# A gated recurrence on one core: one of its six recurrent products of a step computed from three bf16 parts instead of in f32

## The chip, the core and the metric

The kernel runs on one core of a Trainium2 chip. The metric is the device time of one execution in microseconds; lower is better. A core has five engines with queues of their own: TensorE (PE in the profile; PEld is its weight loads), VectorE (DVE), ScalarE (ACT), GpSimd (POOL) and SyncE (SP, here for DMAs alone).

## The reference

For 8 sequences of 512 steps, with 512 inputs and 512 hidden units, all in f32:

```
r, z   = split(sigmoid([x_t, h] @ w_W + w_b))       # w_W: 1024 x 1024
hh     = h @ wh_W + wh_b                            # wh_W: 512 x 512
h_new  = z * h + (1 - z) * tanh(x_t @ wx_W + wx_b + r * hh)
out[:, t] = x_t + h_new
```

The products with x_t don't depend on h and can be made ahead. The three products with h (for r, z and hh) can't: each step needs the h of the step before.

## The kernel before

**Layout.** h lies with its units on partitions: four blocks k of 128 units, of which k = 0, 1 make half A and k = 2, 3 half B. In a product h is the stationary operand (the loaded weights: 128 partitions by 32 columns) and the weight matrix streams past it. 32 columns are a quarter of TensorE's width, so four such products, j = 0 to 3, go to four column groups and leave their results on PSUM partitions 32j to 32j + 31. Of the 32 columns only the 8 of the present step hold h (8 sequences); the others are zero, and a group of four steps (GS) fills one set of PSUM banks, on top of the x part that ScalarE has copied there (`spread`).

**Banks.** The outputs of a step are cut by half of the units and by gate. Bank A (192 columns per j) holds hh, z and r of half A. Bank B (128 columns) holds r and hh of half B. `cs` ("C", 64 columns) holds z of half B. For each bank there are 4 k times 4 j matmuls a step. `wa` and `wb` are the weights of h, read through `wh`.

**Order of a step.** A hand-written string sets TensorE's order:

```
ORDER = "A0 B0 A1 A2 A3 B1 B2 B3 C0 C1 C2 C3"
```

A letter is a bank and a digit a k, four matmuls each. Behind these comes `x_step`: a share of the x products of a later group, 384 columns in four steps of eight and 288 in the other four (`SHARE`), into the tiles `xp` and `eps`.

**The recurrence.** When a bank is done, VectorE turns it back to units on partitions by 32x32 transposes (`turn_r`, `turn_h`, `turn_z`), ScalarE applies the sigmoids, VectorE scans, ScalarE takes the tanh, VectorE scans again:

- `md0` and `md1` are the operands of the first scan (`memory`), interleaved in two slots: hh, then times r plus the x part. Its result is `m`, of 16 elements (8 sequences by 2 slots) for each k, and the tanh of it goes to slot 1 of the old h.
- `hd0` (0, -1, 1 - z) and the three slots of the old h make the second scan (`update`): its third slot is the new h. The tiles `hTA` and `hTB`, eight of each, hold the h of eight steps.

Half A goes ahead: its bank is done after A3, its new h is wanted at A0 and B0 of the next step, that of half B only at A2. POOL adds x to the new h for the output. The x sums that `x_step` needs are made beside (`odd`, `even`, `both`, `more`), three of them on VectorE in steps 2, 3 and 5 of each eight, behind the updates.

**What orders the engines.** The code records its operations in program order (class `Flow`); each engine runs its own in that order, and waits are put where a read, a write or a PSUM bank demands it. All instructions therefore carry one line in the profile (L227). `DVE_FILL` says how many of the first fills go to VectorE instead of POOL. `IDLE` makes two one-element memsets on VectorE at the end of each step (`idle`), and a third stands behind `turn_z(0)`.

Of the kernel before, what the change touches and what calls it, by code (L numbers as in the profile page):

```python
# [8 lines left out]
F32 = mybir.dt.float32  # L9
BF16 = mybir.dt.bfloat16  # L10
AF = mybir.ActivationFunctionType
ALU = mybir.AluOpType
# [10 lines left out]

DVE_FILL = 23
IDLE = 3
ORDER = "A0 B0 A1 A2 A3 B1 B2 B3 C0 C1 C2 C3"

FIRST = "A0 A1 A2 A3 x x x x B0 B1 B2 B3 C0 C1 C2 C3"

BANKS = {"A": 192, "B": 128, "C": 64}  # L30

# [17 lines left out]

XP = {"A": slice(0, 192), "X": slice(192, 320), "C": slice(320, 384), "B": slice(384, 512)}  # L50

# [35 lines left out]
class Flow:  # L87
# [44 lines left out]
    def plan(self):  # L132
# [9 lines left out]
        for i, item in enumerate(self.items):  # L142
# [71 lines left out]
            done.append(snap)  # L214

    def emit(self, tc):

# [21 lines left out]
def tile_cond_rnn_residual(  # L239
# [105 lines left out]
    def wh(bank, k, j):  # L345
        return wa[:, k, j] if bank == "A" else wb[:, k, j, {"C": slice(0, 64), "B": slice(64, 192)}[bank]]

# [7 lines left out]
    NH = 2 * GS  # L355
    hT = [[pair(n, f"hT{n}{i}", 32, 3) for i in range(NH)] for n in "AB"]

    md0 = [[pair(n, f"md0{n}{i}", 32, 2) for i in range(2)] for n in "AB"]
    md1 = [[pair(n, f"md1{n}{i}", 32, 2) for i in range(2)] for n in "AB"]
    hd0 = [[pair(n, f"hd0{n}{i}", B, 3) for i in range(2)] for n in "AB"]  # L360
# [10 lines left out]
    nc.scalar.activation(const.tile([P, 1], F32, name="table"), zeros[:, :1], AF.Sigmoid)  # L371
    for n, t_ in enumerate(hd0[0] + hd0[1] + md0[0] + md0[1] + hT[0] + hT[1]):
# [13 lines left out]
    def state(hf, i, slot=2):  # L386
# [8 lines left out]
         "B": wide[q]["B"][:, : BANKS["B"]],  # L395
         "C": cs[:, HU * q : HU * q + HU]}
# [11 lines left out]

    for t_ in [cs, banks[0]["A"], banks[0]["B"], banks[1]["A"]]:
        mm(t_, none, none[:, :1].broadcast_to([P, t_.shape[1]]), start=True)  # L410
# [42 lines left out]
    def turn_x(g, hf):  # L453

        c0 = XP["X"].start + HU * hf
        nc.vector.transpose(
            md1[hf][g % 2][:, :, :, 1].rearrange("p n c -> p c n"), source(g)[:, c0 : c0 + HU]
        )
# [97 lines left out]
    spread(0, "ABC")  # L556
    for hf in range(2):
# [7 lines left out]
    for i in range(T):  # L565
# [8 lines left out]
        for n in (ORDER if i else FIRST).split():  # L574
            if n == "x":
                take(first[3], 1)
                continue
            bank, k = n[0], int(n[1])
            hs = hT[k // 2][i % NH][:, :, k % 2, 2]
# [9 lines left out]
        def scan(c_, out_, d0, d1):  # L589
# [9 lines left out]
        raw = {  # L599
            "h": (pa[:, :HU], ps["B"][:, HU:]),  # L600
            "z": (pa[:, HU : 2 * HU], ps["C"]),
            "r": (pa[:, 2 * HU :], ps["B"][:, :HU]),
        }
# [9 lines left out]
        def turn_r(hf):  # L613
            tr, _ = turned("r", hf)
            r_done[hf] = act(md0[hf][g % 2][:, rows, :, 1].rearrange("p n c -> p c n"),
                tr,
                AF.Sigmoid,
            )

        def turn_h(hf):  # L620
            inst = nc.vector.transpose(
                md1[hf][g % 2][:, :, :, 0].rearrange("p n c -> p c n"), raw["h"][hf]
            ).ins
# [4 lines left out]
        def turn_z(hf):  # L628
# [10 lines left out]
        ms = [  # L639
            work.tile([P, 2, B, 2], F32, tag=f"m{hf}", name=f"m{hf}_{i}").rearrange("p c n s -> p n c s")  # L640
            for hf in range(2)
        ]

        def memory(hf, q):

            c_ = slice(q, q + 1)
            scan(c_, ms[hf], md0[hf][g % 2][:, rows], md1[hf][g % 2][:, rows])
            act(state(hf, i, 1)[:, :, c_], ms[hf][:, :, c_, 1], AF.Tanh)

# [28 lines left out]
        for hf in range(2):  # L678
            act(state(hf, i + 1, 0), state(hf, i + 1), AF.Copy)
        if i < 3:  # L680
            inst = load_x(i + 1)
# [8 lines left out]
        if o == LAST:  # L690
            if u == 2:
                spread(2 * o + 1, "AB")
                turn_x(2 * o + 1, 0)
                turn_x(2 * o + 1, 1)
            elif u == 3:
                spread(2 * o + 1, "C")
        elif u == 0:
# [8 lines left out]
        elif u == 1:  # L706
            if sums:
                nc.scalar.copy(more[HI], eps)
            spread(2 * o + 1, "BC" if o == 0 else "AC")
        elif u == 2:  # L710
# [25 lines left out]
        elif u == 7 and nxt:  # L736
            if o:
                nc.scalar.copy(odd[LO, XC], reg(GA))
            spread(2 * o + 2, "C")
            turn_x(2 * o + 2, 1)  # L740
# [109 lines left out]
```

## Time and profile before

| | |
|---|---|
| Time, median of 3 runs | 1655.47 us (1655.45 to 1658.25) |
| Profiled execution: time | 1657.46 us |
| Profiled execution: span, first to last instruction | 1655.7 us |
| Granted TensorE clock, mean | 0.999 |
| Busy: PE, PEld | 99%, 91% of the span |
| Busy: DVE, ACT, POOL | 70%, 72%, 18% of the span |
| DMA engines, mean over most of the span | under a tenth busy |

Busy time is the union of the modelled durations of instructions. In a group's row stand the line, engine, operation, output and inputs by the program's names, shapes as partitions by elements, the count, the busy microseconds, the mean nanoseconds of one, and the idle time of the engine just ahead of them with what ended it. In a row of the timeline stand the start and the length in microseconds, the instruction with the number that were merged into it, and in brackets the idle time before it. Each f32 matmul appears in the trace as two matmuls and two weight loads.

### The profile page before, as it was taken

Reading aid. Unit: us, or ns where it says so; the run is one execution under the profiler, and the core shown is the slowest. Engines: PE = TensorE matmul, PEld = TensorE weight load, DVE = VectorE, ACT = ScalarE, POOL = GpSimd, SP = SyncE. Lnnn points to the kernel's source line nnn. Section 1 sums busy time; section 2 is a strip of 40 time slices with the busy share of each in tenths; the row PEclk is TensorE's granted clock in tenths of the full one; section 3 lists DMA queues with packets and bytes.
Section 4 is the critical chain, followed back from the end, with each engine's and each line's share of the span. In section 5 each row is a group of like instructions: output and inputs, shape, how many; then the busy total and the mean of one; then the engine's idle time right before and its main releaser. Section 6 shows DMA issues by size and latency. Waiting matters only on the chain.

```text
span 1655.7 us, 125580 instructions
## 1 busy us (share of the span) xinstructions
PE 1645.6 (99%) x54298; PEld 1500.2 (91%) x54298; DVE 1153.9 (70%) x9194; ACT 1193.8 (72%) x5998; POOL 301.9 (18%) x1279
## 2 busy tenths in 40 slices
PE   9999999999999999999999999999999999999998
PEld 5999999999999999999999999999999999999987
DVE  6776676676766766767667767677676766766765
ACT  3777777777777777777777777777777777777775
POOL 1211111111111111111111111111111111111111
PEclk9999999999999999999999999999999999999999
DMA  4000000000000000000000000000000000000000
GB/s 182 11 18 14 15 15 16 16 14 15 16 15 15 14 16 16 14 14 15 16 15 14 14 17 14 15 14 17 14 14 15 17 14 14 15 17 10 10 10 10
DMA packets 37284, 31.14 MB, mean 19 GB/s; under 512 B 4084, under 2 KB 35060, under 8 KB 36600
## 3 DMA queue, kind: packets, MB, share of 16 engines
q1 hardware_dynamic: 36576, 22.89, 4.5%
q8 instruction: 424, 6.95, 1.7%
q14 instruction: 132, 1.08, 0.2%
q10 hardware_dynamic: 152, 0.22, 0.1%
HBM read 14.70 MB, written 8.39 MB: 14 GB/s over the span
## 4 chain that ended last, share of the span: by engine, by line
PE 99%; DVE 1%; issue 0%; ACT 0%; DVEq 0%; SPq 0%
PE A L227 40%; PE B L227 26%; PE xp L227 18%; PE cs L227 13%; PE eps L227 1%; DVE tr L227 0%; DVE m L227 0%; DVE tz L227 0%; DVE md1B L227 0%; DVE md1A L227 0%; DVE hTA L227 0%; DVE hTB L227 0%; ACT hTB L227 0%; DVE zeros L227 0%; DVE rows L227 0%
## 5 line engine op out<-in xcount | busy, mean ns | idle before, releaser
L227 PE MATMUL A<-wa,hTA 128*32 128x192 f32 x8192 | 559.5, 326 | 2.4 <-DVE hTA L227 2.2
L227 PE MATMUL B<-wb,hTA 128*32 128x128 f32 x8192 | 454.8, 273 | 0.0
L227 PE MATMUL A<-wa,hTB 128*32 128x192 f32 x8192 | 448.6, 326 | 0.0
L227 PEld LDWEIGHTS A<-wa,hTA 128*32 128x32 f32 x8192 | 292.5, 122 | 124.6 <-DVE hTA L227 101.7
L227 DVE STREAM_TRANSPOSE tr<-A 128x64 f32<-128x64 f32 x512 | 128.0, 250 | 367.6 <-PE A L227 367.6
L227 POOL TENSOR_TENSOR ot<-xin,hTB 128x16 f32<-128x16 f32 x495 | 123.8, 250 | 1290.4 <-DVE hTB L227 1290.4
L227 PEld LDWEIGHTS B<-wb,hTA 128*32 128x32 f32 x8192 | 352.6, 122 | 2.8 <-issue 0.3
L227 PE MATMUL B<-wb,hTB 128*32 128x128 f32 x8192 | 339.6, 273 | 0.0
L227 PEld LDWEIGHTS A<-wa,hTB 128*32 128x32 f32 x8192 | 330.4, 122 | 9.1 <-DVE hTB L227 0.2
L227 ACT ACTIVATE md0A<-tr 128x16 f32<-128x16 f32 x512 | 112.4, 219 | 238.5 <-DVE tr L227 238.4
L227 PE MATMUL xp<-tw,sx 128*32 128x384 f32 (+2 forms) x1464 | 269.7, 433 | 0.0
L227 PEld LDWEIGHTS B<-wb,hTB 128*32 128x32 f32 x8192 | 262.3, 122 | 0.2 <-issue 0.2
L227 PE MATMUL cs<-wb,hTB 128*32 128x64 f32 x8192 | 230.3, 219 | 0.4 <-issue 0.3
L227 PE MATMUL cs<-wb,hTA 128*32 128x64 f32 x8192 | 230.2, 219 | 0.0
L227 DVE TENSOR_TENSOR_SCAN hTB<-hd0B,hTB 128x24 f32<-128x24 f32 x1024 | 158.0, 196 | 99.8 <-ACT hTB L227 99.8
L227 PE MATMUL xp<-wx,xin 128*32 128x384 f32 (+4 forms) x1348 | 219.1, 413 | 0.0
L227 PEld LDWEIGHTS cs<-wb,hTA 128*32 128x32 f32 x8192 | 207.5, 122 | 0.0
L227 DVE TENSOR_TENSOR_SCAN hTA<-hd0A,hTA 128x24 f32<-128x24 f32 x1024 | 190.9, 186 | 0.0
L227 ACT ACTIVATE hd0B<-tz 128x16 f32<-128x16 f32 x512 | 115.6, 226 | 94.5 <-DVE tz L227 94.5
L227 PEld LDWEIGHTS cs<-wb,hTB 128*32 128x32 f32 x8192 | 180.2, 122 | 0.7 <-issue 0.7
L227 ACT ACTIVATE hTB<-hTB 128x16 f32<-128x16 f32 x512 | 120.3, 235 | 79.1 <-DVE hTB L227 72.8
L227 ACT ACTIVATE hTA<-m 128x8 f32<-128x8 f32 x1024 | 160.8, 206 | 0.6 <-DVE m L227 0.3
(101 smaller groups left out, 2680.6 us busy)
## 6 DMA issues: line engine op xcount, KB each, us to landing
out_dram<-ot SPq DMA_DIRECT2D x128, 64.0 KB, 1.6
xin<-in_x_dram SPq DMA_DIRECT2D x112, 64.0 KB, 2.4
wx<-in_wx_dram SPq DMA_DIRECT2D x4, 768.0 KB, 7.0
wa<-in_wa_dram SPq DMA_DIRECT2D x4, 384.0 KB, 9.8
wb<-in_wb_dram SPq DMA_DIRECT2D x1, 1152.0 KB, 13.7
xin<-in_x_dram SPq DMA_DIRECT2D x3, 256.0 KB, 3.7
wb<-in_wb_dram SPq DMA_DIRECT2D x1, 384.0 KB, 14.1
head<-in_xh_dram ACTq DMA_DIRECT2D x1, 208.0 KB, 4.7
```

The lines of the kernel that those rows point to most:

```text
L227: inst = getattr(self, item.op, getattr(engine, item.op, None))(*item.args, **item.kw)
```

## The change

Of half B, hh is now computed apart and in bf16; z and r of half B share bank B. In the string of the order "C" has become "H".

- **Products.** h is split into three bf16 parts (their sum is h), side by side as 24 stationary columns (3 parts by 8 sequences). The weights of hh are split as well: the upper half of each f32 word of `wb`, and the same of two remainders, `w2` and `w3`, which POOL makes in step 0. `parts` issues, for each k and j, one matmul with its weight load and two (`kept`) without a load of their own. The streamed operand is every second bf16 of f32 words. The first three steps (`PLAIN`) still use f32 for H.
- **Sums.** The three parts' results lie on 24 partitions of each 32 of `cs`, the bias on the other eight. The product starts afresh each step (`start=k == 0`), so ScalarE no longer fills that bank. The first scan of half B has five slots instead of two (`SL`), 40 elements for each k: three parts, the bias, then times r plus x.
- **Parts of h.** VectorE makes them by two subtractions behind the updates of half B, into `split` (two tiles). The halves of h are one tile of four k, `hT`.
- **Order.** Of half B, z is turned ahead of h's first update, and hh behind it. The two memsets at a step's end are gone (`IDLE = 1`), and `DVE_FILL` is 12.

```diff
-DVE_FILL = 23
-IDLE = 3
-ORDER = "A0 B0 A1 A2 A3 B1 B2 B3 C0 C1 C2 C3"
+DVE_FILL = 12
+IDLE = 1
+ORDER = "A0 B0 A1 A2 A3 B1 B2 B3 H0 H1 H2 H3"
...
-BANKS = {"A": 192, "B": 128, "C": 64}
+BANKS = {"A": 192, "B": 128}
+PLAIN = 3
...
+    def kept(self, out, lhsT, rhs):
+        t = self.nc.tensor
+        return t.add_instruction(
+            mybir.InstMatmult(
...
+                start_tensor_calc=False,
+                stop_tensor_calc=False,
+                tile_size=(128, 32),
+                tile_position=(0, out.offset // 512 // 32 * 32),
+                ldweights=False,
...
+    hs = [const.tile([P, NQ, 64, 3], F32, name=f"hT{i}") for i in range(NH)]
+    split = [const.tile([P, NQ, 3, B], F32, name=f"split{i}") for i in range(2)]
+    w2 = const.tile([P, NQ, NQ, HU], F32, name="w2")
+    w3 = const.tile([P, NQ, NQ, HU], F32, name="w3")
+    SL = [2, 5]
...
+    for t_ in md0[1]:
+        nc.gpsimd.memset(t_[:, :, :, 1:4], 1.0)
...
+    def high(t_):
+        return t_.bitcast(BF16)
+
+    def parts(out_, i, k, j):
+        lhsT = high(split[i % 2])[:, k].rearrange("p u b -> p (u b)")[:, 1::2]
+        for n, t_ in enumerate((wb[:, k, j, 2 * HU :], w2[:, k, j], w3[:, k, j])):
+            if n:
+                nc.tensor.kept(out_, lhsT, high(t_)[:, 1::2])
+            else:
+                mm(out_, lhsT, high(t_)[:, 1::2], start=k == 0)
...
+            nc.scalar.copy(cs[:, :HU], bias[:, XC.stop : 512])
...
-                mm(ps[bank][32 * j : 32 * j + 32, :], hs, wh(bank, k, j))
+                if bank != "H":
+                    mm(ps[bank][32 * j : 32 * j + 32, :], lhsT, wh(bank, k, j))
+                elif i < PLAIN:
+                    mm(cs[32 * j : 32 * j + 24, :HU], lhsT[:, :24], wh(bank, k, j), start=k == 0)
+                else:
+                    parts(cs[32 * j : 32 * j + 24, :HU], i, k, j)
...
         turn_r(1)
+        turn_z(1)
+        update(0, 0)
         turn_h(1)
-        update(0, 0)
-        turn_z(1)
         nc.after(update(0, 1), r_done[1])
...
+        if PLAIN <= i + 1 < T:
+            t_, new = split[(i + 1) % 2], hs[(i + 1) % NH]
+            s1 = B * ((i + 1) % GS)
+            nc.vector.tensor_tensor(
+                t_[:, :, :2].rearrange("p k u b -> p k b u"),
+                new[:, :, s1 : s1 + B, 2].unsqueeze(3).broadcast_to([P, NQ, B, 2]),
+                high(new).rearrange("p k (u n) s -> p k n u s", u=2)[:, :, s1 : s1 + B, :, 5],
+                ALU.subtract,
+            )
+            nc.vector.tensor_tensor(t_[:, :, 2], t_[:, :, 0], high(t_)[:, :, 0, 1::2], ALU.subtract)
+        if i == 0:
+            for to, t_ in ((w2, wb[:, :, :, 2 * HU :]), (w3, w2)):
+                nc.gpsimd.tensor_tensor(to, t_, high(t_)[:, :, :, 1::2], ALU.subtract)
...
-            spread(2 * o + 1, "BC" if o == 0 else "AC")
+            spread(2 * o + 1, "B" if o == 0 else "A")
```

TensorE's queue in step 3 before (weight loads are not listed; here an f32 matmul is one row entry; the last four rows are bank B and C of half A's and half B's h):

```order
L227 MATMUL A0_118<-wa_65,hTA3_70 32x192 x4
L227 MATMUL B0_119<-wb_66,hTA3_70 32x128 x4
L227 MATMUL A0_118<-wa_65,hTA3_70 32x192 x4
L227 MATMUL A0_118<-wa_65,hTB3_78 32x192 x8
L227 MATMUL B0_119<-wb_66,hTA3_70 32x128 x4
L227 MATMUL B0_119<-wb_66,hTB3_78 32x128 x8
L227 MATMUL cs_117<-wb_66,hTA3_70 32x64 x8
L227 MATMUL cs_117<-wb_66,hTB3_78 32x64 x8
```

and in step 4 now, where the three matmuls of one k and one j stand together and the first of the next j follows:

```order
L247 MATMUL A1_116<-wa_65,hT4_71 32x192 x4
L247 MATMUL B1_117<-wb_66,hT4_71 32x128 x4
L247 MATMUL A1_116<-wa_65,hT4_71 32x192 x12
L247 MATMUL B1_117<-wb_66,hT4_71 32x128 x12
L247 MATMUL cs_113<-wb_66,split0_75 24x64
L221 MATMUL cs_113<-w2_77,split0_75 24x64
L221 MATMUL cs_113<-w3_78,split0_75 24x64
L247 MATMUL cs_113<-wb_66,split0_75 24x64
```

A and B are unmoved; behind them 16 entries (32 records) have become 48, three in a row for the same column group, of which every first brings a load.

VectorE's queue of half B before, from bank B's transposes to the end of step 4 (SCALAR_TENSOR_TENSOR is the scan; tz is the transposed z, `tr0` the first of the next step):

```order
L227 STREAM_TRANSPOSE tr1_0_131<-B1_121 128x64
L227 STREAM_TRANSPOSE md1B1_90<-B1_121 128x64
L227 SCALAR_TENSOR_TENSOR hTA5_72<-hd0A0_91,hTA4_71 128x24
L227 STREAM_TRANSPOSE tz1_0_132<-cs_117 128x64
L227 SCALAR_TENSOR_TENSOR hTA5_72<-hd0A0_91,hTA4_71 128x24
L227 SCALAR_TENSOR_TENSOR m1_0_128<-md0B1_86,md1B1_90 128x16 x2
L227 SCALAR_TENSOR_TENSOR hTB5_80<-hd0B0_93,hTB4_79 128x24 x2
L227 TENSOR_TENSOR odd_116<-xp1_123,bias_125 128x384
L227 TENSOR_TENSOR tw1_101<-wx_64,tw0_100 128x384
L227 MEMSET idle_99 128x1 x2
L227 STREAM_TRANSPOSE tr0_1_136<-A1_120 128x64
```

and now, in step 5:

```order
L247 STREAM_TRANSPOSE tr1_1_134<-B1_117 128x64
L247 STREAM_TRANSPOSE tz1_1_135<-B1_117 128x64
L247 SCALAR_TENSOR_TENSOR hT6_73<-hd0A1_88,hT5_72 128x24
L247 STREAM_TRANSPOSE md1B1_86<-cs_113 128x2x4x8
L247 SCALAR_TENSOR_TENSOR hT6_73<-hd0A1_88,hT5_72 128x24
L247 SCALAR_TENSOR_TENSOR m1_1_131<-md0B1_82,md1B1_86 128x40 x2
L247 SCALAR_TENSOR_TENSOR hT6_73<-hd0B1_90,hT5_72 128x24 x2
L247 TENSOR_TENSOR split0_75<-hT6_73 128x4x8x2
L247 TENSOR_TENSOR split0_75<-split0_75 128x4x8
L247 TENSOR_TENSOR tw3_99<-wx_64,tw1_97 128x384
L247 STREAM_TRANSPOSE tr0_2_139<-A1_116 128x64
```

The transpose that waits for `cs` is now that of hh, ahead of the scan m that reads it; m has 40 elements; the two subtractions into `split` stand behind the updates and ahead of what else the step has (the sums `odd` or, here, the one-off `tw`); the two memsets are gone.

More of the change, by code (lines that the diff above doesn't have):

```diff
@@ L371, in tile_cond_rnn_residual @@
     nc.scalar.activation(const.tile([P, 1], F32, name="table"), zeros[:, :1], AF.Sigmoid)
-    for n, t_ in enumerate(hd0[0] + hd0[1] + md0[0] + md0[1] + hT[0] + hT[1]):
+    for n, t_ in enumerate(hd0[0] + hd0[1] + md0[0] + md0[1] + hs):
         (nc.vector if n < DVE_FILL else nc.gpsimd).memset(t_, 0.0)
+    for t_ in md0[1]:
+        nc.gpsimd.memset(t_[:, :, :, 1:4], 1.0)
     for t_ in hd0[0] + hd0[1]:
@@ L406, in mm @@
         )
-    for t_ in [cs, banks[0]["A"], banks[0]["B"], banks[1]["A"]]:
+    for t_ in [banks[0]["A"], banks[0]["B"], banks[1]["A"]]:
         mm(t_, none, none[:, :1].broadcast_to([P, t_.shape[1]]), start=True)
@@ L614, in turn_r @@
             tr, _ = turned("r", hf)
-            r_done[hf] = act(md0[hf][g % 2][:, rows, :, 1].rearrange("p n c -> p c n"),
+            r_done[hf] = act(md0[hf][g % 2][:, rows, :, SL[hf] - 1].rearrange("p n c -> p c n"),
                 tr,
@@ L620, in turn_h @@
         def turn_h(hf):
+            to = md1[hf][g % 2]
             inst = nc.vector.transpose(
-                md1[hf][g % 2][:, :, :, 0].rearrange("p n c -> p c n"), raw["h"][hf]
+                to[:, rows, :, :4].rearrange("p b c s -> p c s b")
+                if hf
+                else to[:, :, :, 0].rearrange("p n c -> p c n"),
+                raw["h"][hf],
             ).ins
@@ L639, in tile_cond_rnn_residual @@
         ms = [
-            work.tile([P, 2, B, 2], F32, tag=f"m{hf}", name=f"m{hf}_{i}").rearrange("p c n s -> p n c s")
+            work.tile([P, 2, B, SL[hf]], F32, tag=f"m{hf}", name=f"m{hf}_{i}").rearrange("p c n s -> p n c s")
             for hf in range(2)
```

38 lines of the change are left out of this document (21 added, 17 removed).

## The prediction

> **What bounds the kernel now.** I read the page first (busy shares, the chain that ended last), then the groups by form, then the timeline of two neighbouring steps.
>
> ```profile
> PE 1645.6 (99%) x54298; PEld 1500.2 (91%) x54298; DVE 1153.9 (70%) x9194; ACT 1193.8 (72%) x5998; POOL 301.9 (18%) x1279
> PE 99%; DVE 1%; issue 0%; ACT 0%; DVEq 0%; SPq 0%
> L227 PE MATMUL A<-wa,hTA 128*32 128x192 f32 x8192 | 559.5, 326 | 2.4 <-DVE hTA L227 2.2
> L227 PE MATMUL cs<-wb,hTB 128*32 128x64 f32 x8192 | 230.3, 219 | 0.4 <-issue 0.3
> ```
>
> TensorE is busy throughout and is the whole chain. A modelled duration (219 ns for 64 columns, 326 for 192) contains the pipeline; its slope, 107/128 = 0.83 ns, is what a column costs. What a whole block costs is seen from starts, here in two steps of the timeline:
>
> ```profile
> 793.88 0.55 PE L227 MATMUL A<-wa,hTA 128*32 128x192 f32 x8
> ...
> 796.05 0.40 PE L227 MATMUL cs<-wb,hTA 128*32 128x64 f32 x15
> 796.27 0.22 PE L227 MATMUL cs<-wb,hTB 128*32 128x64 f32 x1
> 796.28 0.22 PE L227 MATMUL cs<-wb,hTA 128*32 128x64 f32 x1
> ...
> 796.50 0.49 PE L227 MATMUL xp<-tw,sx 128*32 128x384 f32 x1
> ...
> 797.14 0.55 PE L227 MATMUL A<-wa,hTA 128*32 128x192 f32 x8
> ...
> 799.32 0.40 PE L227 MATMUL cs<-wb,hTA 128*32 128x64 f32 x15
> ...
> 799.76 0.41 PE L227 MATMUL xp<-tw,xin 128*32 128x288 f32 x1
> ...
> 800.25 0.55 PE L227 MATMUL A<-wa,hTA 128*32 128x192 f32 x8
> ```
>
> A step runs from A to A: 3.26 us where x has 384 columns, 3.11 where it has 288. The cs block, which the change replaces, lasts 0.45 (796.05 to 796.50). Each f32 matmul is two records (8192 records per half for 512 steps of 8 matmuls), so cs is 32 records; four column groups run side by side, so that is 8 rounds of 0.056, or 64 x 0.83 ns and 2.5 beside. Does a step also wait for the recurrence?
>
> ```profile
> 799.93 0.21 DVE L227 TENSOR_TENSOR_SCAN hTA<-hd0A,hTA 128x24 f32<-128x24 f32 x1
> ...
> 800.20 0.24 PEld L227 LDWEIGHTS A<-wa,hTA 128*32 128x32 f32 x8 [0.26 <-DVE hTA L227]
> ...
> 800.74 0.31 DVE L227 TENSOR_TENSOR_SCAN hTB<-hd0B,hTB 128x24 f32<-128x24 f32 x2 [0.20 <-ACT hTB L227]
> ...
> 801.00 0.30 PEld L227 LDWEIGHTS A<-wa,hTB 128*32 128x32 f32 x8
> ...
> 801.12 0.39 PE L227 MATMUL A<-wa,hTB 128*32 128x192 f32 x4
> ```
>
> In the 288 steps nearly: the weight load of A0 starts 0.06 after the new h of half A is written, and its matmul follows at 800.25 with x just finished. Half B's loads lead by 0.12. How long a step lasts with nothing but the recurrence is seen in the last steps, which have no x work:
>
> ```profile
> 1641.65 0.55 PE L227 MATMUL A<-wa,hTA 128*32 128x192 f32 x8 [0.24 <-DVE hTA L227]
> ...
> 1644.73 0.55 PE L227 MATMUL A<-wa,hTA 128*32 128x192 f32 x8 [0.24 <-DVE hTA L227]
> ...
> 1644.59 0.22 DVE L227 STREAM_TRANSPOSE tz<-cs 128x64 f32<-128x64 f32 x1
> ...
> 1644.83 0.25 DVE L227 TENSOR_TENSOR_SCAN m<-md0B,md1B 128x16 f32<-128x16 f32 x2
> ...
> 1645.53 0.57 PEld L227 LDWEIGHTS A<-wa,hTB 128*32 128x32 f32 x16
> ...
> 1645.64 0.83 PE L227 MATMUL A<-wa,hTB 128*32 128x192 f32 x16
> ...
> 1646.54 0.25 DVE L227 STREAM_TRANSPOSE tr<-A 128x64 f32<-128x64 f32 x1 [0.94 <-PE A L227]
> ...
> 1647.81 0.55 PE L227 MATMUL A<-wa,hTA 128*32 128x192 f32 x8 [0.24 <-DVE hTA L227]
> ```
>
> TensorE idles and the period is 3.08. So each step is the longer of TensorE's work and a floor of 3.08: the 384 steps have 0.18 above the floor, the 288 steps 0.03.
>
> **The change part by part.** *H in place of C.* Per column group and k, one load and three bf16 matmuls of 64 columns stand where two f32 records stood. No steady bf16 matmul exists, but four ran at the start, next to f32 ones:
>
> ```profile
> 2.68 0.37 PE L227 MATMUL A<-none 128*128 128x192 bf16 x1
> 2.84 0.31 PE L227 MATMUL B<-none 128*128 128x128 bf16 x1
> 2.95 0.37 PE L227 MATMUL A<-none 128*128 128x192 bf16 x1
> 3.11 3.67 PE L227 MATMUL xp<-zeros 128*128 128x512 f32 x4
> ```
>
> There bf16 took 0.16 for 192 columns, 0.83 ns each; the f32 records 3.67/2048 = 1.8 ns, about twice that. So everything there went at half the later pace, and against the 0.83 of the steady f32 records I estimate bf16 at 0.42: 64 columns take 27 + 2.5 = 29 ns, twelve rounds 0.35, and H saves 0.097. Bounds: 0.35 from below; from above a bf16 column as dear as an f32 one, 12 x 0.056 = 0.67, since these operands are read with a step of two and no row has that (the four above read a constant). I take 0.35, the only bf16 rows.
>
> *The weight load.* The next k's load stands behind the third matmul and has 29 ns. The loads of A at 801.00 ran under matmuls and held nothing up. With 24 columns instead of 32 I price it at nothing; at worst it shows 12 ns a round, 0.05 a step.
>
> *Side by side or in turn.* Cover: at 796.27 a matmul of half B (later in the program) starts ahead of the last of half A at 796.28. The groups don't wait for each other. [...]
>
> *What the floor leaves.* How many steps gain, and what VectorE's new work costs, comes from these groups and starts:
>
> ```profile
> L227 PE MATMUL xp<-tw,sx 128*32 128x384 f32 x976 | 205.7, 486 | 0.0
> L227 PE MATMUL xp<-wx,xin 128*32 128x384 f32 x732 | 149.9, 486 | 0.0
> L227 PE MATMUL xp<-wx,sx 128*32 128x384 f32 x244 | 51.9, 486 | 0.0
> L227 DVE TENSOR_TENSOR_SCAN m<-md0B,md1B 128x16 f32<-128x16 f32 x1024 | 127.9, 167 | 0.0
> L227 DVE TENSOR_TENSOR_SCAN hTB<-hd0B,hTB 128x24 f32<-128x24 f32 x1024 | 158.0, 196 | 99.8 <-ACT hTB L227 99.8
> L227 DVE TENSOR_TENSOR tw<-wx,tw 128x384 f32<-128x384 f32 x8 | 4.3, 536 | 0.0
> 804.18 0.56 DVE L227 TENSOR_TENSOR even<-xp,both 64x384 f32<-64x384 f32 x1
> ...
> 805.14 0.25 DVE L227 STREAM_TRANSPOSE tr<-A 128x64 f32<-128x64 f32 x1 [0.28 <-PE A L227]
> DVE tz L227 <- PE cs L227: 0.7, 2, 0.5
> L227 POOL TENSOR_TENSOR stepbias<-bias,stepbias 64x384 f32<-64x384 f32 x1 | 1.0, 1019 | 3.3 <-ACT stepbias L227 3.3
> ```
>
> (976 + 732 + 244)/8 = 244 steps have 384 columns, and as many 288 (SHARE alternates four and four). The 384 steps go from 3.265 to 3.17, still above the floor: 244 x 0.097 = 23.7 us. The 288 steps would reach 3.01 but stop at 3.08: 244 x 0.027 = 6.6. The other 24, at both ends, wait for the recurrence already: nothing. Sum 30.3.
>
> *Half B's chain.* hh now comes last. The transpose of cs stands where tz stood; VectorE waited for cs 0.7 us in all, and H ends earlier. But the scan now needs that transpose finished: taking a handover as 0.05 (0.06 from hTA's end to the load at 800.20), it starts at 1644.86 instead of 1644.83 in the last steps shown, 0.03 later. It has 40 elements: from 167 (16) and 196 (24) the slope lies between nothing and 3.6 ns, hence 0 to 0.09; from 196 (24) and 536 (384) it is 0.94, hence 0.023, which I take. New h of half B is 0.053 later (bounds 0.03 to 0.12; a gain is excluded, nothing there shrinks), against a lead of 0.11 to 0.12: free, while the lead lasts. The next in its queue, two updates and the parts, move along. If the load needed half the lead, the dear end would show 0.06 in 244 steps, 15 us.
>
> *Parts on VectorE.* Two subtractions, 64 and 32 elements: by the same line 234 and 204 ns, each behind a handover: 0.54 (bounds 0.49, as two scans of 24, to 1.17, as two tw), less two memsets. Behind them wait the odd or even sum (three steps in eight, 183) and then tr, which starts the next chain. Cover: 0.94 idle ahead of tr in a plain step. In a step with a sum it is 0.40 (804.18 + 0.56 to 805.14, the memsets' place in it), and the sum needn't wait for the second subtraction's end, only for its place, some 0.1: 0.05 + 0.23 + 0.05 + 0.1 = 0.43. Just about covered; the 0.03 missing would be 183 x 0.03 = 5 us at most, left to the range. TensorE needs the parts two microseconds later, behind A and B (800.25 to some 802.4).
>
> *The rest, one answer each.* cs is no longer filled by ScalarE each four steps: off the path. Two subtractions of 1024 on POOL in step 0, by the 1.0 us row some 2.7 each, are needed in step 3, three periods or nine microseconds later. Start-up fills are redistributed under the loads: I take 0, bounds one microsecond either way. In the last step hh being last adds a scan and tanh for a sigmoid, 0.2.
>
> The profiled execution has a span of 1655.7 and a time of 1657.46, 2.0 above the median of 1655.47; both shed 30, so the median goes to **1625**.
>
> **Rivals.**
> 1. *Columns read with a step of two cost as f32 ones.* Place: the moving operands of H. 12 x 0.056 = 0.67, 0.223 more in 509 steps: +114, **1769**. It decides from (446/12 - 2.5)/64 = 0.54 ns a column upwards. For: the f32 records move four bytes per 0.83 ns, and the step doubles the bytes passed over. Against: the bf16 rows, though they read a constant.
> 2. *A column group holds only two matmuls waiting*, and a third blocks the other groups. Then a k takes four rounds: 16 x 0.029 = 0.467, +0.021 x 509 = +10.7, **1666**. For: no run of three exists here. Against: two records per group never blocked.
> [...]
> 4. *The saving is half eaten* by loads that show, the sum steps or half B's lead (0.05 x 244 = 12, 5 to 15 and 15): **1640**.
> 5. *It doesn't save*: H takes 0.35, but the subtractions are 0.09 dearer each, and 183 sum steps lose 0.17 to a late tr, 31 us: **1655**. For: the cover there is spent. Against: they have 64 and 32 elements, and the dear row 384.
>
> **How the numbers follow.** Chances: forecast 0.60 (own range 1616 to 1634: startup, and a floor 0.01 off either way), rival 4 0.13, rival 5 0.04, rival 2 0.06, rival 1 0.13, rival 3 0.04. Leaving out rivals 1 and 3 leaves 0.83 inside; the range goes from 1612 (288 steps passing the floor a little) to 1668. A measurement of this kernel tells 0.2%, 3.3 us, from no change. Faster: 0.60 + 0.13 = 0.73; same: 0.04; slower: 0.06 + 0.13 + 0.04 = 0.23.
>
> **What would show it.** In the changed kernel's timeline the cs block should last 0.35, its matmuls starting 29 ns apart within a group and four groups interleaved; A to A 3.17 in 384 steps and 3.08 in 288 steps, these with TensorE or its loads idle on DVE's h of half A. The scans of 40 should take about 190, the wait of tr for A shrink to some 0.3 a step. I am wrong if cs lasts 0.45 or more, if starts go group by group, or if the 288 steps lengthen past 3.11 with loads waiting for half B.

## The result, and the profile after

The changed kernel takes **1714.0 us** (median of 4 runs, 1713.35 to 1714.81), the kernel before 1655.7 beside it: a ratio of 1.035 (95% interval 1.0331 to 1.0367). It is slower by 58 us, where 1625 was forecast, 30 faster. The product that the change is about became nearly as short as forecast; the loss arose in VectorE's queue.

The page of the changed kernel, busy shares and the chain that ended last:

```profile
PE 1681.7 (98%) x62441; PEld 1274.7 (74%) x46153; DVE 1508.3 (88%) x9177; ACT 1172.9 (69%) x5871; POOL 365.9 (21%) x1286
PE 51%; DVE 43%; ACT 3%; issue 2%; DMA 1%; SPq 0%; DVEq 0%
```

TensorE still shows 98% busy, since busy time counts the modelled duration of a matmul, which covers short gaps (one of A is put at 333 ns where it was 326). The chain tells more: 99% of it was TensorE's, and 43% is VectorE's now.

H, in the timeline of one step (the loads of a k, then its matmuls; L221 are those without a load):

```profile
801.74 0.46 PEld L247 LDWEIGHTS cs<-wb,split 128*24 128x24 bf16 x16
801.85 0.21 PE L247 MATMUL cs<-wb,split 128*24 128x64 bf16 x4
801.88 0.24 PE L221 MATMUL cs<-w,split 128*24 128x64 bf16 x8
801.93 0.21 PE L247 MATMUL cs<-wb,split 128*24 128x64 bf16 x4
...
802.03 0.21 PE L247 MATMUL cs<-wb,split 128*24 128x64 bf16 x4
...
802.12 0.20 PE L247 MATMUL cs<-wb,split 128*24 128x64 bf16 x4
```

One k takes 0.09 us (801.85, 801.93, 802.03, 802.12), three matmuls 30 ns apart in each column group with four groups side by side: 0.36 for the block (0.359 is the median over all steps), where f32 took 0.45.

Two waits of the kernel before (us in total, times, the longest in us), and the row of the loads that need half B's h:

```profile
DVE tr L227 <- PE A L227: 367.6, 507, 1.5
PEld A L227 <- DVE hTA L227: 101.7, 382, 0.7
L227 PEld LDWEIGHTS A<-wa,hTB 128*32 128x32 f32 x8192 | 330.4, 122 | 9.1 <-DVE hTB L227 0.2
```

The same two waits now, and the groups of VectorE that changed (busy, mean ns of one, idle ahead):

```profile
L247 DVE TENSOR_TENSOR_SCAN m<-md0B,md1B 128x40 f32<-128x40 f32 x1024 | 191.7, 229 | 0.0
L247 DVE STREAM_TRANSPOSE md1B<-cs 128x64 f32<-128x64 f32 x512 | 143.8, 281 | 0.0
L247 DVE TENSOR_TENSOR split<-hT 128x64 f32<-128x64 f32 x509 | 142.5, 280 | 17.7
PEld A L247 <- DVE hT L247: 307.7, 899, 1.5
DVE tr L247 <- PE A L247: 54.1, 196, 0.7
```

The wait of tr for TensorE, VectorE's reserve, has shrunk from 367.6 us to 54.1. The loads of A wait 307.7 us for a new h, where they waited 101.7, all of it for half A's. In the changed kernel both halves have one tile name; told apart by their place in the step, 220 us of the 307.7 are waits for half A's h and 87, in 389 steps, for half B's, where the kernel before has 0.2. Where the reserve went is seen in the timeline of a step with a sum (to tr at 801.73), then one without (to 804.91); brackets give the idle time ahead:

```profile
800.24 0.34 DVE L247 TENSOR_TENSOR_SCAN hT<-hd0B,hT 128x24 f32<-128x24 f32 x2 [0.15 <-ACT hT L247]
800.50 0.51 PEld L247 LDWEIGHTS A<-wa,hT 128*32 128x32 f32 x16 [0.24 <-DVE hT L247]
800.61 0.28 DVE L247 TENSOR_TENSOR split<-hT 128x64 f32<-128x64 f32 x1
800.93 0.19 DVE L247 TENSOR_TENSOR split<-split 128x32 f32<-128x32 f32 x1
801.15 0.55 DVE L247 TENSOR_TENSOR odd<-xp,both 64x384 f32<-64x384 f32 x1
801.73 0.25 DVE L247 STREAM_TRANSPOSE tr<-A 128x64 f32<-128x64 f32 x1
802.87 0.27 DVE L247 STREAM_TRANSPOSE md1B<-cs 128x64 f32<-128x64 f32 x1
803.02 0.18 DVE L247 TENSOR_TENSOR_SCAN hT<-hd0A,hT 128x24 f32<-128x24 f32 x1
803.18 0.37 DVE L247 TENSOR_TENSOR_SCAN m<-md0B,md1B 128x40 f32<-128x40 f32 x2
803.71 0.34 DVE L247 TENSOR_TENSOR_SCAN hT<-hd0B,hT 128x24 f32<-128x24 f32 x2 [0.15 <-ACT hT L247]
803.97 0.51 PEld L247 LDWEIGHTS A<-wa,hT 128*32 128x32 f32 x16 [0.23 <-DVE hT L247]
804.91 0.25 DVE L247 STREAM_TRANSPOSE tr<-A 128x64 f32<-128x64 f32 x1 [0.32 <-PE A L247]
```

In the step with a sum, tr at 801.73 has no bracket: VectorE comes straight from the sum. In both, the loads of A for half B's k (x16) wait for half B's new h.

This table is worked out from the trace, from the starts of tr<-A: the median distance to the next one, in ns, over steps 20 to 489, by the step's place in its eight. Places 0 to 3 have 384 columns of x work, 4 to 7 have 288; a sum follows in places 2, 3 and 5. "Floor" is the distance in the last steps, which have no x work. The last column is the median time; the kernel before took 1654.5 to 1657.0 beside these runs.

| kernel | 0, 1 | 2 | 3 | 4 | 5 | 6, 7 | floor | us |
|---|---|---|---|---|---|---|---|---|
| before | 3265 | 3265 | 3265 | 3105 | 3110 | 3110, 3105 | 3082 | 1655 |
| after | 3185 | **3494** | **3480** | 3173 | **3461** | 3189, 3178 | 3169 | 1714 |
| e1, subtractions on GpSimd | 3188, 3183 | 3184 | 3195 | 3176 | 3176 | 3191, 3176 | 3170 | 1659 |
| e2, H in f32 | 3265 | 3265 | 3265 | 3176 | 3180 | 3200, 3180 | 3174 | 1678 |
| e3, before with subtractions | 3265 | 3272 | 3274 | 3089 | **3250** | 3093, 3105 | 3079 | 1663 |
| e8, before, five slots | 3265 | 3265 | 3265 | 3105 | 3110 | 3110, 3105 | 3093 | 1656 |
| e11, before, new order | 3265 | 3265 | 3265 | 3105 | 3110 | 3110, 3105 | 3086 | 1658 |
| e12, both | 3265, 3266 | 3265 | 3265 | 3179 | 3182 | 3195, 3176 | 3177 | 1677 |

So two things happened: the floor rose from 3.08 to 3.17, and the steps with a sum rose to 3.46 to 3.49.

### The profile page after: what moved, and what is told of

Its sections match the earlier page's. It is cut to its first block, busy times and chain, and to the rows that moved or that the text cites. A ratio compares the mean times of both kernels' runs of the same rounds, so it can differ in the third digit from the quotient of the medians.

```text
span 1711.8 us, 125442 instructions
## 1 busy us (share of the span) xinstructions
PE 1681.7 (98%) x62441; PEld 1274.7 (74%) x46153; DVE 1508.3 (88%) x9177; ACT 1172.9 (69%) x5871; POOL 365.9 (21%) x1286
## 4 chain that ended last, share of the span: by engine, by line
PE 51%; DVE 43%; ACT 3%; issue 2%; DMA 1%; SPq 0%; DVEq 0%
PE A L247 28%; PE B L247 12%; DVE m L247 8%; DVE tr L247 7%; DVE hT L247 7%; PE xp L247 7%; DVE split L247 5%; DVE tz L247 5%; PE cs L221 3%; ACT hT L247 3%; DVE md1A L247 2%; DVE md1B L247 2%; DVE xp L247 2%; DVE even L247 2%; DVE odd L247 2%
## 5 line engine op out<-in xcount | busy, mean ns | idle before, releaser
L247 PE MATMUL A<-wa,hT 128*32 128x192 f32 x16384 | 900.5, 333 | 22.4 <-DVE hT L247 6.5
L247 PEld LDWEIGHTS A<-wa,hT 128*32 128x32 f32 x16384 | 484.5, 124 | 345.3 <-DVE hT L247 307.7
L247 PE MATMUL B<-wb,hT 128*32 128x128 f32 x16384 | 635.9, 273 | 0.1
L247 POOL TENSOR_TENSOR ot<-xin,hT 128x16 f32<-128x16 f32 x991 | 278.6, 303 | 1286.9 <-DVE hT L247 1283.9
L247 PEld LDWEIGHTS B<-wb,hT 128*32 128x32 f32 x16384 | 514.3, 122 | 42.4 <-DMA wb<-in_wb_dram 1.1
L247 ACT ACTIVATE hT<-m 128x8 f32<-128x8 f32 x2048 | 340.9, 213 | 195.7 <-DVE m L247 195.3
L247 ACT ACTIVATE hT<-hT 128x16 f32<-128x16 f32 x1024 | 231.1, 226 | 78.9 <-DVE hT L247 74.6
L221 PE MATMUL cs<-w,split 128*24 128x64 bf16 x16288 | 260.3, 192 | 0.0
L247 PE MATMUL cs<-wb,split 128*24 128x64 bf16 x8144 | 245.3, 192 | 0.0
L247 PEld LDWEIGHTS cs<-wb,split 128*24 128x24 bf16 x8144 | 206.2, 93 | 28.7
L247 DVE STREAM_TRANSPOSE tr<-A 128x64 f32<-128x64 f32 x512 | 128.1, 250 | 65.6 <-PE A L247 54.1
```

The costliest lines, as they stand in the source:

```text
L221: return t.add_instruction(mybir.InstMatmult(name=self.nc.get_next_instruction_name(), ins=[t.lower_ap(rhs), t.lower_ap(lhsT)], outs=[t.lo ...
L247: inst = getattr(self, item.op, getattr(engine, item.op, None))(*item.args, **item.kw)
```

## The experiments

V is the theory that VectorE carries the whole loss, in these two ways: half B's longer chain, and the subtractions in the steps with a sum. Every expectation tells its rivals.

**e1: the subtractions on GpSimd.**

```diff
-            nc.vector.tensor_tensor(            # split, first
+            nc.gpsimd.tensor_tensor(
-            nc.vector.tensor_tensor(t_[:, :, 2], ...   # split, second
+            nc.gpsimd.tensor_tensor(t_[:, :, 2], ...
```

> The changed kernel with both subtractions that make the parts of h on GpSimd instead of VectorE. Theory V (VectorE): in the three sum steps of eight the period (3.46 to 3.49 us) is VectorE's own loop, and 0.28 + 0.19 us of subtractions with their handovers are the excess. Taken off, these steps fall to the period of the other five, 3.17 to 3.19, and the time to 1714 - 3/8 x 512 x 0.30 = 1656 (1648 to 1662). Rival O (the new order, the merged tile of h or the shared bank make new waits): the sum steps stay near 3.47 and the time above 1700. Rival G (GpSimd is too slow): H waits for the parts, more than 3.25 in every step, above 1690.

Measured: 1658.98 us, 1.0028 of before (1.0016 to 1.0039). The waits and GpSimd's group:

```profile
DVE tr L247 <- PE A L247: 286.8, 507, 0.9
PEld A L247 <- DVE hT L247: 238.6, 810, 1.5
L247 POOL TENSOR_TENSOR split<-hT 128x64 f32<-128x64 f32 x509 | 168.4, 331 | 1011.4 <-DVE hT L247 1011.4
```

The steps with a sum are like all others (3.18 to 3.20), and tr waits for TensorE again. So of the 58 us, 54 are the place of the two subtractions on VectorE (58.3 less the 4.5 by which this run is slower than the kernel before beside it). GpSimd is slower at it (331 ns where VectorE took 280), and hides it. But the loads' wait for h stays, and the floor with it.

**e2: H in f32, without subtractions.** Only the first three steps of the changed kernel use f32; here all do. Every fourth step's hh of half B leaves out h by this, so it is read for its time alone.

```diff
-PLAIN = 3
+PLAIN = 512
```

> The changed kernel with hh of half B in f32 in every step (24 columns, no parts, no subtractions; every fourth step's hh of half B leaves out h, since its eight columns are not among the 24), all else as changed: five slots, order, merged tile, shared bank. Theory V: only the longer chain of half B is left, a floor of 3.17. Steps with 384 columns are bound by TensorE at 3.265 as in the kernel before, steps with 288 at 3.17 instead of 3.108: 1655.5 + 244 x 0.063 = 1671 (1664 to 1677). Rival T (the bf16 matmuls cost more than the cs block shows): back to 1655. Rival O: above 1690.

Measured: 1678.2 us, 1.0145 (1.013 to 1.016), a microsecond above the range. The floor of 3.17 is there without any bf16 matmul and without a subtraction; the 384 steps are at 3.265 again, TensorE's own time with f32.

**e3: the kernel before, with the two subtractions added.** They read a tile of zeros and nobody uses their result; they stand where the changed kernel has them, and the memsets at the step's end are gone.

```diff
-IDLE = 3
+IDLE = 1
...
+            nc.vector.tensor_tensor(t_[:, :, :2]..., hx..., hx..., ALU.subtract)   # 128 x 64
+            nc.vector.tensor_tensor(t_[:, :, 2], t_[:, :, 0], ..., ALU.subtract)    # 128 x 32
```

> The kernel before with the two subtractions alone added on VectorE, at the place and with the wait they have in the changed kernel, on a tile of zeros (their result is not used), and the two memsets gone. Theory V: plain steps have 0.94 us of VectorE idle and don't change; a sum step becomes VectorE's loop of 2.12 + 1.15 = 3.27 to 3.29: u=5 (288 columns) grows by 0.16 to 0.18, u=2 and u=3 by 0 to 0.03. 61 x 0.16 to 61 x 0.24: 1665 to 1671. So most of the loss in the sum steps comes only where the longer chain of half B is added to it. Rival O: 1655.

Measured: 1662.73, 1.0049 (1.0032 to 1.0066), two microseconds below the range: place 5 came to 3.25 and not 3.27. The same subtractions cost 8 us here and 54 in the changed kernel. A step with a sum in the timeline of e3:

```profile
801.73 0.31 DVE L227 TENSOR_TENSOR_SCAN hTB<-hd0B,hTB 128x24 f32<-128x24 f32 x2 [0.20 <-ACT hTB L227]
802.07 0.29 DVE L227 TENSOR_TENSOR split<-hx 128x64 f32<-128x64 f32 x1
802.39 0.19 DVE L227 TENSOR_TENSOR split<-split 128x32 f32<-128x32 f32 x1
802.60 0.55 DVE L227 TENSOR_TENSOR odd<-xp,both 64x384 f32<-64x384 f32 x1
803.18 0.25 DVE L227 STREAM_TRANSPOSE tr<-A 128x64 f32<-128x64 f32 x1
```

From half B's update to the next tr it is 1.45 here and 1.49 in the changed kernel (800.24 to 801.73): the same tail. What differs is the way from tr to half B's update: 1.83 here (the tr ahead of these rows starts at 799.90), 1.98 there (801.73 to 803.71). 1.83 + 1.45 = 3.28 is only just over the 3.265 that TensorE needs anyway in places 2 and 3, so it shows in place 5 alone (3.25 for 3.11). 1.98 + 1.49 = 3.47 shows in all three, against a TensorE that now needs less. The two costs lie in one loop.

**e4: the changed kernel with the old turns**: hh of half B turned ahead of half A's first update, z behind it.

```diff
         turn_r(1)
-        turn_z(1)
-        update(0, 0)
         turn_h(1)
+        update(0, 0)
+        turn_z(1)
```

> The changed kernel with the turns of half B in the old order (hh ahead of the first update, z behind it). Theory V: the first scan of half B no longer waits for its transpose (0.08 us earlier), but the transposes ahead of the update of half A are longer (0.28 instead of 0.21), which moves half A by up to 0.07: plain steps 3.12 to 3.17, sum steps shorter by as much; 1690 to 1714. Rival O (the order is the cause): 1655 to 1670.

Measured: 1707.6, 1.0318 (1.0303 to 1.0334). The turn now waits for cs, which TensorE finishes last, and holds up half A's update (the turn starts 1.01 behind tr, median, and 0.88 in the kernel before): steps and floor of 3.215. But the steps behind a late sum, where cs is ready in time, went down to 3.08 (place 4) and 3.10 (place 6). So order matters for the floor, and it can't be put back by itself.

**e5, e6, e7: shortening half B's chain in e1.** I first thought that the long turn itself was the cause, and tried to get it out of the way: the second update of half A behind the first m scan (e5), the turn in two halves of 32 columns (e6), and both (e7).

```diff
 e5        memory(1, 0)
          +nc.after(update(0, 1), r_done[1])
           memory(1, 1)
 e6       -turn_h(1)        +turn_h(1, 0)       # 32 columns; turn_h(1, 1) behind memory(1, 0)
 e7       -turn_h(1)        +turn_h(1, 0); turn_h(1, 1); then as e5
```

> The subtractions stay on GpSimd here and in the next two, so all three are to be read against 1659 us, where every step took 3.17 to 3.19. Edit: the second update of half A stands behind the first m scan of half B on VectorE. Theory V (the loop through half B is bound by VectorE's own queue: tr of A, ..., first update of A, the turn of hh of B 0.28, the first m scan of 40 elements 0.23, tanh, update of B, then the loads A2): the scan is held by the end of the turn (start plus 0.28 plus 0.04) as much as by the update ahead of it (0.17), so it comes forward by 0.00 to 0.04: 1640 to 1659, most likely 1655. Rival P (from 3.17 on TensorE is the bound): nothing moves, 1658 to 1662. Rival A (half A's chain is as tight): the later second update delays A1 by up to 0.19: 1665 to 1700.

> Edit against the 1659 us version: the turn of hh of B is made in two halves of 32 columns, the second one behind the first m scan. Theory V: the first scan comes 0.05 to 0.10 earlier, the second some 0.05 to 0.10 later, so A2's loads come earlier and A3's later: 1640 to 1665, most likely 1650; a gain of any size says that the long turn was in the path. Rival P: 1658 to 1664.

> Edit against the 1659 us version: both halves of the turn back to back, then the first m scan, then the second update of half A, then the second scan. Theory V: the first scan comes about 0.10 earlier and the second is about where it was; the steps go to 3.08 to 3.15 where TensorE has less, 1625 to 1650, most likely 1640, faster than before. Rival A: A1 waits for the update that now stands 0.2 later, 1660 to 1700. Rival P: 1658 to 1664.

Measured: 1704.3 (1.0297, 1.028 to 1.0314), 1700.2 (1.0275, 1.0259 to 1.029) and 1673.0 (1.0108, 1.0093 to 1.0124): three misses, all slower than e1's 1659. The timeline of e5 says why:

```profile
801.23 0.28 DVE L247 STREAM_TRANSPOSE md1B<-cs 128x64 f32<-128x64 f32 x1
801.61 0.24 DVE L247 TENSOR_TENSOR_SCAN m<-md0B,md1B 128x40 f32<-128x40 f32 x1
801.77 0.18 DVE L247 TENSOR_TENSOR_SCAN hT<-hd0A,hT 128x24 f32<-128x24 f32 x1
```

The scan starts 0.10 behind the turn's end; with the update between them it was 0.04 (802.87 + 0.27 to 803.18). The update moved was not in the way: it stood in the wait for the turn, and without it that wait is longer. So half B's first update starts 2.05 behind tr where e1 has 1.98 (medians here and below), and the steps take at least 3.24 for 3.18. In e6 a half of the turn takes 219 ns, hardly less than a whole one of 281, so cutting it adds work to the same queue: half B's second update starts 2.38 behind tr for 2.11, and the loads for k = 3 wait for it in 506 steps, in e1 in none. In e7 half B's first update is back at 1.99, and six of the eight places stay at e1's 3.18 to 3.20. Its loss lies in places 1 and 2 (3.27 and 3.24): the second update still comes 0.11 late, with it come ScalarE's copies (`both`, and the x part that it spreads into A), and the sigmoid of r that stands behind them starts 0.37 and 0.34 behind tr for 0.28. e5 and e6 lose there in the same way. Rival A, the later second update of half A, isn't borne out: loads of A for k = 1 waited 9 times in e5 and in e7, for k = 0 some 450 times.

**e8: the kernel before with five slots.** Half B's m tiles as wide as in the changed kernel: hh in slot 0, three slots that add zero, x in slot 4. Nothing else differs in a step.

```diff
+    SL = [2, 5]
-    md1 = [[pair(n, f"md1{n}{i}", 32, 2) for i in range(2)] for n in "AB"]
+    md1 = [[pair(n, f"md1{n}{i}", 32, SL[n == "B"]) for i in range(2)] for n in "AB"]
```

(md0 and m likewise.)

> The kernel before with half B's m tiles widened from two slots to five (hh in slot 0, three slots of zeros kept with factor one, x in slot 4): the turn writes every 20 bytes in place of every 8, the scan has 40 elements in place of 16, and nothing else changes; the result is the same. Theory V (turn 0.216 to 0.28 and scan 0.167 to 0.23 are what lengthened half B's chain): about 0.10 to 0.13 on a lead of 0.11, and where the turn stands ahead of the first update of half A up to 0.065 there: the 288-column steps go from 3.11 to 3.12 to 3.18, the 384-column steps stay at 3.265: 1656 to 1672, most likely 1662. Rival O (the new order of the queue, not the durations, raised the floor): 1653 to 1656.

Measured: 1655.98, 1.0005 (0.9995 to 1.0014): no change, where V's range (from 1656) meets rival O's (to 1656). Width alone raises the floor by 0.01 and no other step. V as I had it, durations alone, fell; order had to come in.

**e11 and e12: the order alone, and with the width.** e11 is the kernel before with the changed kernel's places: z and r of half B in one bank, hh in f32 as the last block, the turns in the new order. e12 is the same with e8's five slots. With before and e8 they are the four corners.

```diff
-XP = {..., "C": slice(320, 384), "B": slice(384, 512)}
+XP = {..., "B": slice(320, 448), "C": slice(448, 512)}
...
-        turn_h(1)
-        update(0, 0)
         turn_z(1)
+        update(0, 0)
+        turn_h(1)
```

> The kernel before with the changed kernel's places alone: z and r of half B in one bank, hh of half B in f32 in its own bank as the last block, and on VectorE the turn of z ahead of the first update of half A and the turn of hh behind it. Two-slot tiles, no subtractions. Theory V2 (order and width add up; one of them fits in the lead of 0.11): the first m scan of half B is held by the end of the turn, 0.22 plus 0.04 behind its start, 0.02 to 0.04 later than before, so the floor stays at 3.08 to 3.10: 1652 to 1660, most likely 1656. Rival O (the order alone raises the floor to 3.17): 288-column steps at 3.18, 1671 to 1679.

> The same with half B's tiles of five slots: both parts together, still f32 and without subtractions. Theory V2: the turn is 0.28 and holds the scan 0.08 longer, the scans of 40 elements cost 0.07 more: floor 3.16 to 3.18, 288-column steps 3.17 to 3.19 and 384-column steps 3.265: 1671 to 1680, most likely 1676. If it stays under 1662, the floor of 3.17 has a cause that neither names (the strided columns of h, the bf16 matmuls' own latency).

Measured: e11 1657.9, 1.0004 (0.9995 to 1.0014), no change; e12 1676.9, 1.0117 (1.0102 to 1.0132). Neither alone costs anything that can be measured, both together 20 us. The chain of half B in the timelines of the kernel before, e8, e11 and e12, from tr to the first m scan to the update:

```profile
802.03 0.25 DVE L227 STREAM_TRANSPOSE tr<-A 128x64 f32<-128x64 f32 x1 [0.97 <-PE A L227]
803.40 0.25 DVE L227 TENSOR_TENSOR_SCAN m<-md0B,md1B 128x16 f32<-128x16 f32 x2
803.84 0.31 DVE L227 TENSOR_TENSOR_SCAN hTB<-hd0B,hTB 128x24 f32<-128x24 f32 x2 [0.20 <-ACT hTB L227]
```

```profile
804.58 0.25 DVE L227 STREAM_TRANSPOSE tr<-A 128x64 f32<-128x64 f32 x1 [0.18 <-PE A L227]
805.97 0.35 DVE L227 TENSOR_TENSOR_SCAN m<-md0B,md1B 128x40 f32<-128x40 f32 x2
806.47 0.34 DVE L227 TENSOR_TENSOR_SCAN hTB<-hd0B,hTB 128x24 f32<-128x24 f32 x2
```

```profile
804.33 0.25 DVE L227 STREAM_TRANSPOSE tr<-A 128x64 f32<-128x64 f32 x1 [0.23 <-PE A L227]
805.74 0.28 DVE L227 TENSOR_TENSOR_SCAN m<-md0B,md1B 128x16 f32<-128x16 f32 x2
806.22 0.31 DVE L227 TENSOR_TENSOR_SCAN hTB<-hd0B,hTB 128x24 f32<-128x24 f32 x2 [0.19 <-ACT hTB L227]
```

```profile
804.20 0.25 DVE L227 STREAM_TRANSPOSE tr<-A 128x64 f32<-128x64 f32 x1 [0.26 <-PE A L227]
805.66 0.37 DVE L227 TENSOR_TENSOR_SCAN m<-md0B,md1B 128x40 f32<-128x40 f32 x2
806.19 0.34 DVE L227 TENSOR_TENSOR_SCAN hTB<-hd0B,hTB 128x24 f32<-128x24 f32 x2 [0.15 <-ACT hTB L227]
```

From tr to half B's first update the medians over steps 20 to 489 are 1.81 in the kernel before, 1.88 in e8, 1.87 in e11 and 1.98 in e12, as in the changed kernel. The width adds 0.07, the order 0.05, both together 0.17, more than their sum: the longer turn (282 ns for 230) holds up the scan only where it stands one instruction ahead of it. The time follows from the rest of the loop. From that update to the next tr it takes 1.20 where half B sets the period (the median of e1 and of the changed kernel, and of the last steps of e2 and e12). So the loop through half B is 3.02 in the kernel before, 0.07 under the floor of 3.08 and 0.09 under the 3.11 of the 288 steps; with 1.88 and 1.87 it is 3.09 and 3.07, which still fits but for 0.01 in e8's floor; with 1.98 it is 3.18, and that is the new floor.

**e9 and e10: z taken out of r's bank again.** To get hh early and keep bf16: r alone, then H, then z in the unused columns of the other group's bank B, with the old turns, and with ScalarE filling that part of the bank every four steps again. The subtractions are on GpSimd in e9, on VectorE in e10.

```diff
-ORDER = "A0 B0 A1 A2 A3 B1 B2 B3 H0 H1 H2 H3"
+ORDER = "A0 B0 A1 A2 A3 B1 B2 B3 H0 H1 H2 H3 C0 C1 C2 C3"
-BANKS = {"A": 192, "B": 128}
+BANKS = {"A": 192, "B": 64}
...
+         "C": wide[1 - q]["B"][:, HU : 2 * HU],
```

> The changed kernel with z of half B taken out of the bank of r again: r alone in bank B (64 columns), then hh in its own bank, then z last (64 columns, in the unused part of the other group's bank B); on VectorE the turn of hh stands ahead of the first update of half A again and the turn of z behind it, as in the kernel before. The subtractions are on GpSimd. Theory V2 (half B's chain grew by 0.17 because two things come together: the turn of hh, now 0.28, stands with only one instruction between it and the first m scan, 0.08; and the scan of 40 elements costs 0.07 more; either alone fits in the lead of 0.11): the floor goes back to 3.09, the 288-column steps to 3.10 to 3.13 and the 384-column steps, TensorE's, to 3.17 to 3.19: mean 3.135 in place of 3.19, 1628, with 1620 to 1645 for the parts coming too late for an earlier hh: faster than before. Rival W (the wider scan and turn are enough, wherever they stand): 1650 to 1660 as with GpSimd and the new order.

> The same with the subtractions on VectorE, as the changed kernel has them: the fourth corner beside the changed kernel (1714), the one with GpSimd (1659) and the run above. Theory V2: in the sum steps VectorE's own loop stays, 3.46 less at most 0.08, against 3.14 without: 3/8 of 488 steps times 0.24 to 0.32 is 44 to 58 us more than the run above: 1665 to 1695, most likely 1676. Rival D (with the shorter chain of half B the subtractions fit, as in the kernel before, where they cost 8 us): 1630 to 1642.

Measured: 2030.9 (1.2273, 1.2251 to 1.2294) and 2034.6 (1.2305, 1.2285 to 1.2326). Both expectations missed, and neither run tests the theory, since TensorE ran into something else. The page of e9 (its last row here is queue q8, which the page names instruction, with packets and MB), its timeline inside H, and that queue in the kernel before:

```profile
PE 1804.8 (89%) x78825; PEld 1534.3 (75%) x62537; DVE 1274.6 (63%) x8159; ACT 1228.6 (60%) x5999; POOL 579.5 (28%) x2304
PE 88%; issue 11%; DVE 1%; ACT 0%; DVEq 0%; SPq 0%
q8 instruction: 552, 9.04, 1.8%
801.81 0.35 PEld L247 LDWEIGHTS cs<-wb,split 128*24 128x24 bf16 x14 [0.51 <-issue]
q8 instruction: 424, 6.95, 1.7%
```

"issue" is time in which TensorE waited for nothing that the profile shows: in the middle of H, with its operands long there, the loads stood still for 0.51, and elsewhere for up to 1.5. The trace tells what the stalls go with. e9 has 78825 + 62537 = 141362 records on TensorE, 256 for each of the 552 packets of q8; the kernel before has 108596, 256 for each of 424. In e9 TensorE starts nothing for more than 0.3 us 589 times, 376 us in all; 540 of the 588 distances between these stalls are 256 records exactly, and half of the stalls end 1.33 to 1.45 us behind the end of a packet. The kernel before has 41 such pauses, and of their distances one is 256. So I read the stalls as TensorE waiting for its next instructions. Without the stalls e9 would be at some 1658, by estimate (its span of 2034 less 376): it would use up a packet in 3.0 us, and they came one in 3.6. H alone has as many records as in f32 (16 loads and 48 matmuls for 32 and 32); the block for z adds 64 in each step, and by this reading those don't come in time. With z and r in one bank the changed kernel has 108594 records, and none of its pauses lie 256 apart.

No version of the changed kernel beat the kernel before; the nearest is e1, 0.3% slower.

## Why the prediction was wrong, step by step

- **H in place of C: right.** 0.36 for 0.35. A streamed bf16 column, read with a step of two, cost 0.43 ns ((30 - 2.5)/64) where 0.42 was estimated, which buries rival 1. The weight load showed 0.01 of the block at most; no run shows the 12 ns a round, 0.05 a step, that I gave as its worst. The 3.18 for 3.17 in the 384 steps is no proof of it: half B's new loop of 3.18 stands at the same height there.
- **Side by side: right.** The four first matmuls of a k (801.85) start ahead of the eight others (from 801.88), though in the program each group's three stand together. The groups neither go in turn (rival 3, chance 0.04) nor block each other (rival 2). Across column groups, then, the matmuls of H don't start in the order of the program; the ends in the trace are modelled and show nothing of it.
- **Half B's chain: the first step that failed.** I priced it 0.053 later, with 0.12 as the upper bound, against a lead of 0.11 to 0.12. It was 0.17, against 0.07 to 0.09. Three terms were mis-sized. The start of the m scan moved by 0.08, not 0.03 (1.37 behind tr in the kernel before, 803.40 less 802.03; 1.45 in the changed one): I gave the turn of hh the duration of the others, but with a step of five slots it takes 281 ns and not 216 to 225, and the scan must wait for its end. The wider scans moved the update by another 0.09, not 0.023 (from 0.44 to 0.53 behind the scan's start): 40 elements take 229 ns, not 190. My own line, 0.94 ns an element from 196 at 24, gives 211, a rise of 0.044 over the 167 of 16 elements; I had added its slope alone to the 167. And the lead: half B's loads start 0.12 ahead of their matmul, but half A's, which wait for their h, still start 0.05 ahead of theirs (800.20 and 800.25), so not all of it is time to spare. The loop through half B had 0.07 to spare in the steps without x work and 0.09 in the 288 steps, by the sums behind e12. "Free, while the lead lasts" was the right condition; e8 and e11 show it holding for each part, e12 failing for the sum. The price: 244 steps at 3.175 to 3.18 in place of the 3.08 forecast, about 24 us, where the dear end that I gave was 15.
- **Parts on VectorE: the second step that failed.** I set 0.43 against a cover of 0.40. Three terms were too small: the first subtraction took 0.28 and not 0.23; the sum started only behind the end of the second (801.15, after 800.93 + 0.19), 0.22 behind its start and not 0.10; and the 0.17 of half B's chain stands ahead of both, in the same queue, and I never added it. The sum started 0.91 behind half B's update instead of 0.34 (803.84 to 804.18 before). That is 0.57, and with the 0.17 it is 0.74 against 0.40. The 0.34 missing agree with 3.46 against 3.11 in place 5. 183 such steps with 0.28 to 0.31 more than their neighbours make 54 us; e1 gives 54.
- **Which rival came.** Rival 5, a late tr in the 183 sum steps, named the place and had 0.17 for 0.28 to 0.31 and a chance of 0.04. It took the loss to end at the kernel before, since it let the plain steps keep their gain. Both failures together were no rival at all, though one delays what the other leaves no cover for.
- **The sign that I named** was right: 288 steps past 3.11 with loads waiting for half B.

The account against the kernel before, by the table: 244 steps gain 0.08 (20 us), 244 lose 0.07 (17), the 24 without x work lose 0.09 (2), which is nearly nothing, as e1's span of 1656.9 against 1655.7 says; the subtractions add 54. By the times beside each other e1 is 4.5 slower and not 1: the span of 1655.7 belongs to an execution of 1657.46, while the median beside e1 is 1654.5. Where the difference of some 3 us comes from is not shown.

## What to carry to other kernels

Where several small delays fall into one queue, add them up in that queue before comparing the sum with what there is to spare: each alone fitted into 0.07 to 0.09, and an experiment that adds one of them alone shows nothing. A busy engine hides which engine sets the period; the loop is found by adding up starts from one instruction to its next turn, and here it ran through VectorE, with TensorE at 98%. Work that an engine "has time for" on the mean may stand in just the steps that have none: put it on the engine whose result nobody waits for, even if it takes longer there.

## What the runs showed of the hardware

- **The step of a write counted for this transpose.** The same transpose, in the same place, took 230 ns with its 64 elements 8 bytes apart and 282 with 20 bytes (e11 and e12); the ones of x into the same tiles went from 222 and 206 to 278 and 260, while those into half A's tiles, still 8 bytes apart, stayed at 220 to 224. I had not looked at the step for this transpose. Why the wider one costs more is not shown.

```profile
L227 DVE STREAM_TRANSPOSE md1B<-cs 128x64 f32<-128x64 f32 x512 | 117.9, 230 | 0.3 <-PE cs L227 0.2
L227 DVE STREAM_TRANSPOSE md1B<-cs 128x64 f32<-128x64 f32 x512 | 144.6, 282 | 0.6 <-PE cs L227 0.6
```

- **A scan right behind the transpose that it reads starts later**: 0.10 behind the turn's end with nothing between, 0.04 with an update between (e5). It is no rule for every pair: the second subtraction reads the first and starts 0.04 behind it with nothing between (800.61 + 0.28 to 800.93). The cause stays open.
- **bf16 columns 4 bytes apart cost 0.43 ns each** (30 ns for 64 columns; 0.09 for three matmuls, the load and the first start of a k included), about half of the 0.83 of an f32 record's column.
- **TensorE stood still once in 256 records in e9**, for 376 us in all, where q8 moved one packet for 256 records and one in 3.6 us (median); in the kernel before, with one packet in 3.9 us, there was no such pattern (41 pauses, one of their distances 256). That it waited for its own instructions is my reading of this. What keeps the packets 3.6 us apart stays open.
